# A three-pass graph kernel whose first pass gathers raw node rows and normalises them per edge, in place of a table of normalised rows

## The chip, the cores and the metric

The kernel runs on one core of one Trainium2 chip. The metric is device time in microseconds (us), the median of several runs. Beside the timed runs there is one profiled execution, whose trace gives the start and length of every instruction. The engines are named as in the profile: PE (matrix products; PEld is its weight load), DVE (vector), ACT (activations), POOL (GpSimd), SP (issues transfers). Indirect transfers ("gathers": 128 rows picked by 128 indices) are issued by POOL.

## The reference

Two graph layers over 30,000 nodes of 128 features and 960,000 edges sorted by destination. Each layer normalises the node rows and applies a Relu before its messages.

```python
h = jnp.maximum(_layernorm(x, axis=-1), 0.0)
x = x + _L0_gnn_ref(h, edge_weight1, basis1, coeff1, bias1, basis2, coeff2, bias2,
                    src, dst, edge_type_32)      # two convolutions, Relu between
h = jnp.maximum(_layernorm(x, axis=-1), 0.0)
x = x + _L1_gnn_ref(h, edge_index, edge_type_4, Wk, bk, Wq, bq, Wv, bv, Ws, b)
```

A convolution of layer 0 sends, along each edge, the source row times the weight of the edge's type (a mix of eight basis matrices by `coeff`), times the edge's own weight, and sums at the destination. Layer 1 sends `sigmoid(k[dst] + q[src]) * v[src]`.

## The kernel before, in words

The edges are cut into 7,500 tiles of 128; three tiles make a group (G = 3), five groups a step (S = 5), five steps a load stage (SB = 5); below, "stage" in the estimates means one step of five groups. There are 500 steps per pass, 100 load stages, and NI = 5 long blocks, unrolled. Edges run from the highest destination to the lowest, so that a group's destinations lie in a window of W = 32 nodes above its first one. Sums are kept in SBUF in `agg`, one column per node (128 x 30360).

**Preparation** (lines 186 to 312). `agg` is set to zero on POOL (L177). 25 steps of 1,200 nodes load x on SP (L230), take statistics on DVE (bn_stats L236, then four small steps L239 to L244), a square root on ACT (L249), reciprocal and shift on DVE (L251, L253), and scale and Relu the rows on ACT (L265), two rows in ten on POOL (L260, L263) from the sixth step on; the rows are stored to the table h0 in HBM (L267). In between, five chunks subtract each group's first destination from its destinations (L205), store these positions to `reld` (L214) and take their lowest and highest (L213, L217). From these a count of violations is summed through PE into `flag` and loaded into a register of every engine (L312). If it is zero, the sorted path runs (L1079), otherwise a general path.

**Sorted path**, three passes of `edge_pass` (L404), each with 7,500 gathers:

- Passes 1 and 2 (`rel_body`, L479). Per group: three gathers of source rows into one slot of `hg` (L598 to L600, issued through L118; five slots); `sb` = position one-hot (`hits`, L592) times the edge's eight coefficients (L604, DVE); three products on PE into `pa` (L608), the first of which waits for all three gathers; a copy by ACT to `ab` (L619). Per step: 16 products with the bases (`bases_out`, L562), emitted after the next step's second group; window sums into `agg` (L477, DVE). In pass 1 also the edge types' one-hot `oh` (L526), their product with the coefficients (L531) and the scaling by the edge weights (`ce`, L541). Pass 1 also turns finished blocks of 120 nodes into h1 (`after_first`, L731), and prepares codes for pass 3 (`codes`, L866).
- Pass 2 gathers from h1, pass 3 (`gate_body`, L643) gathers query and value rows and multiplies them out.

The order inside the blocks is the order of emission, written by hand (`tc.manual_schedule()`); small steps are put beside given groups by `todo` and `beside`. Every engine works its instructions in that order. A slot is reused when what read and wrote it is done.

Of the kernel before, what the change touches and what calls it, by code (L numbers as in the profile page):

```python
# [52 lines left out]
CH = 5  # L53
PX, KX = 120, 10
BUSY = 5
# [17 lines left out]
def kernel(  # L73
# [103 lines left out]
    nc.gpsimd.memset(agg, 0.0)  # L177
# [4 lines left out]
    bas1 = state.tile([P, B, D], F32, name="bas1")  # L182
# [3 lines left out]
    CT, CG = NT // CH, NGR // CH  # L186
    STEPS = N // (PX * KX)
    with tc.tile_pool(name="prep", bufs=2) as prep, tc.tile_pool(name="pre", bufs=4) as pre, \
            tc.tile_pool(name="prep_ps", bufs=1, space=PSUM) as prep_ps:
        lo = prep.tile([TP, CH], F32, name="lo", bufs=1)  # L190
        hi = prep.tile([TP, CH], F32, name="hi", bufs=1)

        def edge_chunk(c):

            ts = slice(c * CT, (c + 1) * CT)
            fi = prep.tile([TP, CG], I32, name="fi")
            dch = prep.tile([TP, CT], I32, name="dch")
            rch = prep.tile([TP, CT], BF16, name="rch")

            def load():  # L200
                nc.sync.dma_start(fi, rows_of(first[c * CG:(c + 1) * CG], TP))
                nc.sync.dma_start(dch, dst[:, ts])

            def less():
                nc.vector.tensor_tensor(  # L205
                    rch.rearrange("p (g j) -> p g j", j=G),
                    dch.rearrange("p (g j) -> p g j", j=G),
                    fi.unsqueeze(2).to_broadcast([TP, CG, G]),
                    ALU.subtract,
                )  # L210

            def lowest():
                nc.vector.tensor_reduce(lo[:, c:c + 1], rch, AX.X, ALU.min)  # L213
                nc.scalar.dma_start(reld[:, ts], rch)  # L214

            def highest():
                nc.vector.tensor_reduce(hi[:, c:c + 1], rch, AX.X, ALU.max)  # L217

            return load, less, lowest, highest

        xts, sums, scales, shifts = {}, {}, {}, {}

        def rows(array, i):
            some = array[i * (PX * KX):(i + 1) * (PX * KX), :]
            return some.rearrange("(p k) d -> p k d", k=KX)

        def load(i):
            if i < STEPS:
                xts[i] = pre.tile([PX, KX, D], F32, name="xt", bufs=5)
                nc.sync.dma_start(xts[i], rows(x, i))  # L230

        def statistics(i):
            if i < STEPS:
                st = pre.tile([PX, KX, 6], F32, name="st")
                for k in range(KX):
                    nc.vector.bn_stats(st[:, k, :], xts[i][:, k, :])  # L236
                even, odd = (st[:, :, q * 3 + 1:q * 3 + 3] for q in range(2))
                sums[i] = pre.tile([PX, KX, 2], F32, name="mv")
                nc.vector.tensor_add(sums[i], even, odd)  # L239
                apart = pre.tile([PX, KX], F32, name="apart")  # L240
                nc.vector.tensor_sub(apart, even[:, :, 0], odd[:, :, 0])
                nc.vector.scalar_tensor_tensor(apart, apart, D / 4.0, apart,
                                               op0=ALU.mult, op1=ALU.mult)
                nc.vector.tensor_add(sums[i][:, :, 1], sums[i][:, :, 1], apart)  # L244

        def scale(i):
            if i < STEPS:
                scales[i] = pre.tile([PX, KX], F32, name="rs")
                nc.scalar.activation(scales[i], sums[i][:, :, 1], AF.Sqrt, scale=1.0 / D,  # L249
                                     bias=eps[:PX])  # L250
                nc.vector.reciprocal(scales[i], scales[i])  # L251
                shifts[i] = pre.tile([PX, KX], F32, name="off")
                nc.vector.scalar_tensor_tensor(shifts[i], sums[i][:, :, 0], -0.5, scales[i],  # L253
                                               op0=ALU.mult, op1=ALU.mult)

        def results(i):
            h = pre.tile([PX, KX, D], F32, name="h", bufs=3)
            own = KX if i < BUSY else KX - 2
            for k in range(own, KX):
                nc.gpsimd.tensor_scalar(h[:, k, :], xts[i][:, k, :], scales[i][:, k:k + 1],  # L260
                                        shifts[i][:, k:k + 1], op0=ALU.mult, op1=ALU.add)
            if own < KX:
                nc.gpsimd.tensor_scalar(h[:, own:], h[:, own:], 0.0, None, op0=ALU.max)  # L263
            for k in range(own):
                nc.scalar.activation(h[:, k, :], xts[i][:, k, :], AF.Relu,  # L265
                                     scale=scales[i][:, k:k + 1], bias=shifts[i][:, k:k + 1])
            nc.scalar.dma_start(rows(h0, i), h)  # L267

        def edge_steps():
            ready = edge_chunk(0)  # L270
            yield ready[0]
            for c in range(CH):
                following = edge_chunk(c + 1) if c + 1 < CH else ()
                yield from following[:1]
                yield from ready[1:]
                ready = following

        with tc.manual_schedule():
            between = edge_steps()
            for i in range(4):  # L280
                load(i)
            statistics(0)
            scale(0)
            statistics(1)
            for i in range(STEPS):
                load(i + 4)
                if i == STEPS - 5:
                    nc.sync.dma_start(bas1, basis1.rearrange("b d f -> d b f"))
                statistics(i + 2)
                scale(i + 1)  # L290
                next(between, int)()
                results(i)
            for step_ in between:
                step_()
        bad = prep.tile([TP, 2, CH], F32, name="bad", bufs=1)
        nc.vector.tensor_scalar(bad[:, 0, :], lo, 0.0, None, op0=ALU.is_lt)
        nc.vector.tensor_scalar(bad[:, 1, :], hi, float(W - 1), None, op0=ALU.is_gt)
        nbad = prep.tile([TP, 1], F32, name="nbad", bufs=1)
        nc.vector.tensor_reduce(nbad, bad, AX.XY, ALU.add)
        at = prep.tile([NI, NG], I32, name="at", bufs=1)  # L300
        nc.sync.dma_start(at, first.rearrange("(i g) -> i g", i=NI))
        even = prep.tile([NI, NG], F32, name="even", bufs=1)
        nc.gpsimd.iota(even, pattern=[[-NPI // NG, NG]], base=N + LAG - LEAD - W,
                       channel_multiplier=-NPI, allow_small_or_imprecise_dtypes=True)
        nc.vector.tensor_tensor(even, at, even, ALU.is_gt)
        late = prep.tile([NI, 1], F32, name="late", bufs=1)
        nc.vector.tensor_reduce(late, even, AX.X, ALU.add)
        nc.vector.tensor_add(nbad[:NI], nbad[:NI], late)
        pbad = prep_ps.tile([1, 1], F32, name="pbad")
        nc.tensor.matmul(pbad, lhsT=nbad, rhs=ones[:TP], start=True, stop=True)  # L310
        nc.vector.tensor_copy(flag, pbad)
    n_bad = nc.values_load(flag[0:1, 0:1], min_val=0, max_val=2 * CH * TP + NGR)  # L312
# [44 lines left out]
    def sorted_path():  # L357
# [7 lines left out]
        with ExitStack() as all_:  # L365
# [38 lines left out]
            def edge_pass(name, body, after, banks, extra=None, finish=None, apart=None):  # L404


                with ExitStack() as held:
                    weights = held.enter_context(tc.tile_pool(name=f"{name}_w", bufs=1))
                    steps, start = after(weights), body(weights)
                    with tc.tile_pool(name=f"{name}_io", bufs=4) as io, \  # L410
# [10 lines left out]
                        for i in range(NI):  # L421
                            with tc.manual_schedule():
                                todo = {}
                                for n, step_ in extra(i, npool) if extra else ():
                                    todo.setdefault(n, []).append(step_)
# [53 lines left out]
            def rel_body(table, weights, second):  # L479
# [3 lines left out]
                def start(npool):  # L483
                    bas = weights
                    if second:
                        bas = npool.tile([P, B, D], F32, name="bas")
                        nc.scalar.dma_start(bas, weights.rearrange("b d f -> d b f"))
# [15 lines left out]
                def body(bas, pos, hits, i, io, pool, ps, cp, iw, ic, beside):  # L503
# [5 lines left out]
                    def loads(k):  # L509
                        stage[k] = [stage_tile(io, "idx", src, I32, i, k),  # L510
                                    stage_tile(io, "relc", reld, BF16, i, k),
                                    firsts(io, i, k)]
                        if not second:
                            stage[k].append(
                                stage_tile(io, "nrm", norm, F32, i, k, 4 * TQ - S * G))
# [55 lines left out]
                    if second:  # L571
                        kept(0)
                        kept(1)
                    else:
                        types(0)
                        onehot(0)
                        coefficients(0)
                        types(1)
                        onehot(1)
# [564 lines left out]
```

## Time and profile before

| | us |
|---|---|
| median of 3 runs | 28303.81 (28299.06 to 28304.94) |
| the profiled execution | 28301.08 |
| its span | 28299.3 |
| busy: PE, DVE, ACT, POOL | 19712.1, 11533.8, 3619.0, 21324.8 |
| gathers into hg (passes 1 and 2) | 15000 x 945 ns |
| gathers into qv (pass 3) | 7500 x 945 ns |
| granted PE clock, mean over the span | 0.751 |

The span runs from the first to the last instruction. A row of a group of instructions names the line, the engine, the operation and the tiles, out from in, with the shapes; then the count, the busy time, the mean of one in ns, and the idle time of the engine before them with what ended it ("issue" is time in which the engine waited for nothing that the profile shows). A row in order of time has the start, the length, engine, line, operation, tiles and count, and in brackets the idle time before. A queue's own rows end in q (SPq, ACTq).

### The profile page before, as it was taken

Reading aid. Unit: us, or ns where it says so; the run is one execution under the profiler, and the core shown is the slowest. Engines: PE = TensorE matmul, PEld = TensorE weight load, DVE = VectorE, ACT = ScalarE, POOL = GpSimd, SP = SyncE. Lnnn points to the kernel's source line nnn. Section 1 sums busy time; section 2 is a strip of 40 time slices with the busy share of each in tenths; the row PEclk is TensorE's granted clock in tenths of the full one; section 3 lists DMA queues with packets and bytes.
Section 4 is the critical chain, followed back from the end, with each engine's and each line's share of the span. In section 5 each row is a group of like instructions: output and inputs, shape, how many; then the busy total and the mean of one; then the engine's idle time right before and its main releaser. Section 6 shows DMA issues by size and latency. Waiting matters only on the chain.

```text
span 28299.3 us, 269530 instructions
## 1 busy us (share of the span) xinstructions
PE 19712.1 (70%) x79371; PEld 15934.8 (56%) x79371; DVE 11533.8 (41%) x23522; ACT 3619.0 (13%) x9761; POOL 21324.8 (75%) x22574
## 2 busy tenths in 40 slices
PE   5666666666666666666666666667777777777777
PEld 4555555555555444444444444457777777777676
DVE  4333333333333333333333333344444444444444
ACT  2111111111111111111111111111111111111111
POOL 7777777777777777777777777777777777777777
PEclk9888888888888888888888888875555555555555
DMA  4222222222222222222222222235555555555554
GB/s 126 75 75 83 75 81 77 75 84 74 77 81 75 74 77 76 76 77 77 77 77 77 77 77 76 76 101 151 151 152 152 151 152 152 152 151 152 152 152 146
DMA packets 1982721, 2911.61 MB, mean 103 GB/s; under 512 B 680564, under 2 KB 1364077, under 8 KB 1981277
## 3 DMA queue, kind: packets, MB, share of 16 engines
q0 software_dynamic: 840000, 1967.52, 24.7%
q1 hardware_dynamic: 740695, 656.22, 7.5%
q10 hardware_dynamic: 400582, 270.54, 3.6%
q8 instruction: 672, 11.01, 0.2%
q14 instruction: 772, 6.32, 0.1%
HBM read 2621.06 MB, written 271.38 MB: 102 GB/s over the span
## 4 chain that ended last, share of the span: by engine, by line
POOL 36%; DMA 31%; issue 23%; PE 6%; DVE 2%; DVEq 0%; POOLq 0%; ACT 0%; SPq 0%; ACTq 0%
DMA hg<-h,idx 24%; POOL hg L118 22%; POOL qv L118 14%; DMA qv<-qvtab,qi 7%; PE pa L608 3%; PE pb L562 2%; DVE pk L715 1%; DVE msg L687 1%; DVE agg L477 0%; PE bank L806 0%; PE cp L531 0%; DVEq L464 0%; DVE sb L604 0%; POOLq L118 0%; PE po L689 0%
## 5 line engine op out<-in xcount | busy, mean ns | idle before, releaser
L118 POOL DMA_INDIRECT hg<-h,idx x15000 | 14168.1, 945 | 4592.9 <-issue 3623.0
L608 PE MATMUL pa<-sb,hg 128*128 128x256 f32 x30000 | 8716.0, 435 | 6192.4 <-DMA hg<-h,idx 4946.6
L608 PEld LDWEIGHTS pa<-sb,hg 128*128 128x128 f32 x30000 | 5983.7, 212 | 8490.9 <-issue 5744.2
L118 POOL DMA_INDIRECT qv<-qvtab,qi x7500 | 7090.1, 945 | 2312.9 <-issue 2055.2
L689 PE MATMUL po<-sel,msg 128*128 128x32 f32 x15000 | 3653.5, 400 | 2206.9 <-DVE msg L687 2202.0
L689 PEld LDWEIGHTS po<-sel,msg 128*128 128x128 f32 x15000 | 3401.0, 327 | 2799.8 <-DVE msg L687 2795.0
L678 PE MATMUL pk<-kw,oh 128*128 128x128 f32 x15000 | 4029.8, 442 | 11.4 <-DMA kw<-ktab 11.4
L619 ACT COPY ab<-pa 128x256 f32<-128x256 f32 x5000 | 1860.3, 372 | 16488.9 <-PE pa L608 16205.4
L678 PEld LDWEIGHTS pk<-kw,oh 128*128 128x128 f32 x15000 | 3504.1, 334 | 11.6 <-issue 11.6
L715 DVE TENSOR_TENSOR pk<-pk,qv 128x384 f32<-128x384 f32 x2500 | 1415.7, 566 | 5017.4 <-DMA qv<-qvtab,qi 4627.3
L477 DVE TENSOR_TENSOR agg<-agg,pb 128x32 f32 x5000 | 937.4, 187 | 4488.3 <-PE pb L562 4342.8
L562 PE MATMUL pb<-ab,bas 128*128 128x160 f32 (+1 forms) x12080 | 2705.0, 387 | 0.9 <-ACT ab L619 0.9
L562 PEld LDWEIGHTS pb<-ab,bas 128*128 128x128 f32 x12080 | 2352.3, 230 | 399.0 <-issue 58.6
L604 DVE TENSOR_TENSOR sb<-hits,ce 128x768 f32<-128x768 f32 x2500 | 2295.1, 950 | 192.7 <-issue 167.3
L604 DVE TENSOR_TENSOR sb<-cp,ce 128x768 f32<-128x768 f32 x2500 | 2308.1, 948 | 17.2
L716 ACT ACTIVATE pk<-pk 128x384 f32<-128x384 f32 x2500 | 1187.5, 475 | 8056.7 <-DVE pk L715 8056.7
L789 DVE BATCH_NORM_STATS2 st<-bank 120x6 f32<-120x128 f32 x253 | 75.6, 299 | 3339.8 <-PE bank L786 3339.8
L687 DVE TENSOR_TENSOR msg<-pk,qv 128x384 f32<-128x384 f32 x2500 | 1369.3, 548 | 0.0
L665 DVE TENSOR_TENSOR oh<-kb,cp 128x1920 f32<-128x1920 bf16 x500 | 1072.3, 2145 | 7.8 <-DMA kb<-kcode 7.8
L817 DVE TENSOR_TENSOR kt<-bank,ball 120x512 f32<-120x512 f32 x253 | 175.0, 692 | 1795.4 <-PE bank L806 1795.1
L806 PE MATMUL bank<-wall,hT 128*120 128x512 f32 x1518 | 836.1, 665 | 0.0
L592 DVE TENSOR_TENSOR hits<-cp,relc 128x480 f32<-128x480 f32 x500 | 330.7, 661 | 693.1 <-PE cp L531 691.0
(87 smaller groups left out, 5371.5 us busy)
## 6 DMA issues: line engine op xcount, KB each, us to landing
hg<-h,idx POOLq DMA_INDIRECT x15000
kb<-kcode SPq DMA_DIRECT2D x500, 480.0 KB
kw<-ktab SPq DMA_DIRECT2D x2500, 64.0 KB
er<-in_et_row SPq DMA_DIRECT2D x500, 256.0 KB
qvtab<-qvt ACTq DMA_DIRECT2D x250, 480.0 KB
qv<-qvtab,qi POOLq DMA_INDIRECT x7500
ktab<-kt ACTq DMA_DIRECT2D x253, 240.0 KB
ce<-ce ACTq DMA_DIRECT2D x500, 60.0 KB
```

Source lines behind the costliest of these rows:

```text
L118: return nc.gpsimd.indirect_dma_start(out=to, out_offset=None, in_=table, in_offset=bass.IndirectOffsetOnAxis(ap=idx, axis=0))
L477: nc.vector.tensor_add(to, to, po[:, at + g, :])
L562: nc.tensor.matmul(po[z][:, of].rearrange("p s w -> p (s w)"), lhsT=bas[:, b, :], rhs=ab[z][:, b, of].rearrange("p s w -> p (s w)"), start ...
L604: nc.vector.tensor_mul(sb, hits[:, of, :].unsqueeze(2).to_broadcast([TP, G, B, W]), ce[s][:, of, :].unsqueeze(3).to_broadcast([TP, G, B, W]))
L608: product = nc.tensor.matmul(pa.rearrange("p b w -> p (b w)"), lhsT=hg[:, j, :], rhs=sb[:, j].rearrange("p b w -> p (b w)"), start=(j == 0 ...
L619: nc.scalar.copy(ab[z][:, :, s % A * S + g, :], pa)
L665: nc.vector.tensor_tensor(oh[s], kb[s], ic.unsqueeze(2).to_broadcast([P, S, GE]), ALU.is_equal)
L678: nc.tensor.matmul(pk[n][:, j, :], lhsT=oh[n // S][:, n % S, j * TP:(j + 1) * TP], rhs=kw[n], start=True, stop=True)
L687: nc.vector.tensor_mul(msg, pk[n], qv[n][:, :, 1, :])
L689: nc.tensor.matmul(po[s][:, g, :], lhsT=msg[:, j, :], rhs=sel[s][:, g * G + j, :], start=(j == 0), stop=(j == G - 1))
L715: nc.vector.tensor_add(pk[n], pk[n], qv[n][:, :, 0, :])
L716: nc.scalar.activation(pk[n], pk[n], AF.Sigmoid)
```

## The change

The preparation goes, and with it the table h0 on the sorted path. Pass 1 gathers rows of x itself, into seven slots instead of five. Its groups are handled in two batches of a step, groups 0 and 1, and groups 2, 3 and 4. When a group's rows are there, DVE takes their statistics; when the batch's last are, DVE combines them, ACT takes the square root of the spread for all the batch's tiles, DVE makes reciprocal and shift, and ACT scales and Relus the rows in place, three tiles at a time, each three followed by the group's three products and ACT's copy. The first product no longer waits for all rows of its group in pass 1. Positions are made at the load stages, 75 columns at a time, from loads of the destinations and of the groups' first destinations; they are used from SBUF in pass 1 and stored for the later passes. Their extremes are kept per load stage. `agg` is cleared by DVE in 25 pieces beside the first 25 groups. The count of violations is made in pass 2 beside its 62nd to 64th group; it is loaded into registers between passes 2 and 3. The sorted path always runs, and the general path follows after it if the count is above zero; that path now makes h0 for itself.

```diff
+BATCHES = {1: (0, 1), 4: (2, 3, 4)}
+CLEARED = 25
...
-    nc.gpsimd.memset(agg, 0.0)
...
-    with tc.tile_pool(name="prep", bufs=2) as prep, tc.tile_pool(name="pre", bufs=4) as pre, \
-            tc.tile_pool(name="prep_ps", bufs=1, space=PSUM) as prep_ps:
...
-    n_bad = nc.values_load(flag[0:1, 0:1], min_val=0, max_val=2 * CH * TP + NGR)
+    STAGES = NI * NQ
+    lo = state.tile([TP, STAGES], F32, name="lo")
+    hi = state.tile([TP, STAGES], F32, name="hi")
...
                     def loads(k):
...
+                            dch = stage_tile(io, "dch", dst, I32, i, k)
+                            fi = io.tile([TP, NGS], I32, name="fi")
+                            n = i * NG + k * NGS
+                            nc.sync.dma_start(fi, rows_of(first[n:n + NGS], TP))
...
+                    def positions(k):
+                        dch, fi = stage[k][1]
+                        relc = io.tile([TP, NTS], BF16, name="relc")
+                        nc.vector.tensor_tensor(
+                            relc.rearrange("p (g j) -> p g j", j=G),
+                            dch.rearrange("p (g j) -> p g j", j=G),
+                            fi.unsqueeze(2).to_broadcast([TP, NGS, G]), ALU.subtract)
+                        stage[k][1] = relc
+                        n = i * NQ + k
+                        nc.scalar.dma_start(reld[:, n * NTS:(n + 1) * NTS], relc)
+                        nc.vector.tensor_reduce(lo[:, n:n + 1], relc, AX.X, ALU.min)
+                        nc.vector.tensor_reduce(hi[:, n:n + 1], relc, AX.X, ALU.max)
+
+                    def statistics(st, hg):
+                        for j in range(G):
+                            nc.vector.bn_stats(st[:, j, :], hg[:, j, :])
+
+                    def spread(st, n):
+                        even, odd = (st[:, :n, q * 3 + 1:q * 3 + 3] for q in range(2))
+                        both = pool.tile([TP, 3 * G, 2], F32, name="both")[:, :n]
+                        nc.vector.tensor_add(both, even, odd)
+                        apart = pool.tile([TP, 3 * G], F32, name="apart")[:, :n]
+                        nc.vector.tensor_sub(apart, even[:, :, 0], odd[:, :, 0])
+                        nc.vector.scalar_tensor_tensor(apart, apart, D / 4.0, apart,
+                                                       op0=ALU.mult, op1=ALU.mult)
+                        nc.vector.tensor_add(both[:, :, 1], both[:, :, 1], apart)
+                        rs = pool.tile([TP, 3 * G], F32, name="rs")[:, :n]
+                        nc.scalar.activation(rs, both[:, :, 1], AF.Sqrt, scale=1.0 / D,
+                                             bias=eps[:TP])
+                        return both, rs
+
+                    def shifted(both, rs, n):
+                        nc.vector.reciprocal(rs, rs)
+                        off = pool.tile([TP, 3 * G], F32, name="off")[:, :n]
+                        nc.vector.scalar_tensor_tensor(off, both[:, :, 0], -0.5, rs,
+                                                       op0=ALU.mult, op1=ALU.mult)
+                        return off
...
+                        if not second and s % SB == SB - 1 and k + 1 < NQ:
+                            positions(k + 1)
...
                         for g in range(S):
-                            hg = pool.tile([TP, G, D], F32, name="hg", bufs=5)
+                            hg = pool.tile([TP, G, D], F32, name="hg", bufs=5 if second else 7)
                             rows = [gather(hg[:, j, :], table, idx[:, t0 + j:t0 + j + 1])
                                     for j in range(G)]
+                            ready = BATCHES.get(g)
+                            if not second:
+                                if g in (0, 2):
+                                    st = pool.tile([TP, 3 * G, 6], F32, name="st")
+                                at = (g if g < 2 else g - 2) * G
+                                statistics(st[:, at:at + G], hg)
+                                if ready:
+                                    both, rs = spread(st, at + G)
                             sb = pool.tile([TP, G, B, W], F32, name="sb", bufs=4)
...
+                            held[g] = hg, rows, sb
+                            if second:
+                                product(g, *held[g])
+                            elif ready:
+                                off = shifted(both, rs, at + G)
+                                for q, one in enumerate(ready):
+                                    for j in range(G):
+                                        n = q * G + j
+                                        mine = held[one][0][:, j, :]
+                                        nc.scalar.activation(mine, mine, AF.Relu,
+                                                             scale=rs[:, n:n + 1],
+                                                             bias=off[:, n:n + 1])
+                                    product(one, *held[one])
...
+            def clear(q):
+
+                size = NX // CLEARED
+                low = NX - (q + 1) * size if q + 1 < CLEARED else 0
+                return lambda: nc.vector.memset(agg[:, low:NX - q * size], 0.0)
...
+                return [(61, count), (62, ahead), (63, whole)]
...
-            edge_pass("c1", rel_body(h0, bas1, False), after_first, 2, codes, finish_later)
-            edge_pass("c2", rel_body(h1, basis[1], True), after_second, 2, apart=6)
+            edge_pass("c1", rel_body(x, basis[0], False), after_first, 2, codes, finish_later)
+            edge_pass("c2", rel_body(h1, basis[1], True), after_second, 2, verdict, apart=6)
             both.close()
+            n_bad = nc.values_load(flag[0:1, 0:1], min_val=0,
+                                   max_val=2 * STAGES * TP + NGR)
             edge_pass("g", lambda weights: lambda cps: gate_body, after_third, 1)
...
-    with tc.If(n_bad == 0) as cmp:
-        sorted_path()
-    with cmp.Else():
+    n_bad = sorted_path()
+    with tc.If(n_bad > 0):
         any_path()
```

`product` holds the three products and ACT's copy that stood in the loop before.

## The prediction

> **What bounds the kernel now.** I read the page first, then a table by stage, cut at the first and last gather of each pass, then what GpSimd (POOL) waits for in pass 1, then the instructions in order of time around the places that the change touches. From the page: the span, the chain that ended last, and the costliest group.
>
> ```profile
> span 28299.3 us, 269530 instructions
> ...
> POOL 36%; DMA 31%; issue 23%; PE 6%; DVE 2%; DVEq 0%; POOLq 0%; ACT 0%; SPq 0%; ACTq 0%
> ...
> L118 POOL DMA_INDIRECT hg<-h,idx x15000 | 14168.1, 945 | 4592.9 <-issue 3623.0
> ```
>
> Gathers (POOL issues, their DMAs, POOL's "issue" gap) carry the chain. By stage (length, then busy time and instructions of PE, weight loads, DVE, ACT, POOL, then the granted clock):
>
> ```profile
> 0.00:128.50 128.50, 0.19 (x2) 0.09 (x2) 97.80 (x427) 90.96 (x236) 66.64 (x74) 1.00 0.88 299
> 128.50:9505.70 9377.20, 6114.54 (x27478) 5056.94 (x27478) 3514.24 (x7312) 1045.26 (x2999) 7091.77 (x7500) 0.86 0.28 78
> 9505.70:9518.50 12.80, 4.97 (x28) 3.85 (x28) 4.86 (x14) 2.00 (x7) 0.00 (x0) 0.91 0.24 56
> 9518.50:18880.20 9361.70, 6403.51 (x21554) 4286.52 (x21555) 3625.65 (x7235) 1190.84 (x3498) 7076.29 (x7500) 0.89 0.28 77
> ```
>
> Each pass issues 7,500 gathers. In pass 1 they start at a mean pitch of (9504.74 - 128.50)/7499 = 1.2503 us: 0.946 busy and 0.304 of gap. What POOL waited for there (total, times, longest):
>
> ```profile
> POOL hg L118 <- issue: 1808.2, 5933, 0.3
> POOL hg L118 <- DMA hg<-h,idx: 390.1, 1280, 0.3
> POOL hg L118 <- PE pa L608: 47.5, 156, 0.3
> POOL hg L118 <- PE cp L531: 34.7, 114, 0.3
> POOL hg L118 <- DMA h<-h: 9.2, 1, 9.2
> ```
>
> Apart from the first gather (9.2 us, for the normalised rows) no wait is longer than the fixed gap of 0.3 us: buffers, PE, DVE and ACT never hold POOL up. So the span is the time before the first gather, three lots of 7,500 pitches, two transitions and a tail. Only what moves the first gather, the pitch or a transition moves the end. POOL's rows there:
>
> ```profile
> 128.50 1.15 POOL L118 DMA_INDIRECT hg<-h,idx  x1 [9.25 <-DMA h<-h]
> 129.96 0.94 POOL L118 DMA_INDIRECT hg<-h,idx  x1 [0.30 <-issue]
> ...
> 9504.74 0.94 POOL L118 DMA_INDIRECT hg<-h,idx  x1 [0.30 <-issue]
> 9518.55 0.94 POOL L118 DMA_INDIRECT hg<-h,idx  x1 [12.88 <-DVE sb L604]
> ```
>
> **Start.** The table of normalised rows goes, and with it all work up to 128.50 us: 25 loads and 25 stores of 600 KB, statistics, ACT's and POOL's scaling, five large position chunks. The first gather then needs only its indices, SP's first DMA. SP issued its first at 0.74 us, an index load takes 0.36 us to issue, and the last small store before pass 2 was issued by 9515.83, 2.7 us before the gather that it released. 0.74 + 0.36 + 2.7 = 3.8; POOL's constants end at 2.2. I take 4.0, bounds 3.5 to 6.5 (the first 600 KB load was used at 6.11). **-124.5 us**, between -125.0 and -122.0.
>
> **POOL in pass 1.** It loses a memset (25.4 us, which lay beside the old preparation) and gains no data work. A slot of hg must now also be free of DVE's and ACT's accesses, so there are more waits in POOL's queue. The trace shows one extra wait instruction per group there already (17 ns, once 804 ns of waiting at 310.96), with the next gather still 1.25 us after the one before; the first eight gathers had none, at the same pitch. I take 0; dearer only if a wait outlasts about 0.8 us.
>
> **ACT in pass 1**, per stage of 5 groups = 15 gathers = 18.75 us. Added: 15 Relus and two square roots. From the preparation and the steady part of pass 1 (start, length):
>
> ```profile
> 86.96 3.17 ACT L265 ACTIVATE h<-xt,off,rs 120x128 f32<-120x128 f32 x8
> ...
> 326.01 1.53 PE L608 MATMUL pa<-sb,hg 128*128 128x256 f32 x6 [3.04 <-DMA hg<-h,idx]
> ...
> 327.58 0.37 ACT L619 COPY ab<-pa 128x256 f32<-128x256 f32 x1 [4.20 <-PE pa L608]
> 327.85 0.40 ACT L746 ACTIVATE r<-agg,b1c 128x120 f32<-128x120 f32 x1
> ...
> 341.25 2.90 PE L608 MATMUL pa<-sb,hg 128*128 128x256 f32 x6 [3.20 <-DMA hg<-h,idx]
> ```
>
> Eight Relus in 3.17 us at 479 ns each are a pitch of 0.385. The written order is three Relus, PE's products, ACT's copy of the sum, then the next group's Relus, so ACT and PE take turns. At full clock: first Relu 0.48 + 0.05 + products 1.57 to the copy's start + 0.27 to ACT's next = 2.4 us. At half clock the products took 2.90: 3.8 us. Five groups, plus per batch about 0.9 us (square root 0.30, then DVE's reciprocal 0.21 and shift 0.17 with their gaps), plus 0.85 for ACT's stores and other steps: 12.0 + 1.8 + 0.85 = **14.6 us of 18.75** at full clock, **21.6** at half. The granted clock of pass 1 is 0.86, half clock 28% of the time: 5 x 2.8 + 2.65 = 16.6. It fits. Behind a late batch stand the next batch's square root, hence DVE's shift and whatever DVE has queued behind it; POOL feels that only when a slot stays full.
>
> **Slots.** Count from a stage's first gather. Group 4's last row lands at 14 x 1.25 + 2.2 = 19.7 (the row issued at 323.80 met its product at 326.01). Statistics 0.3, DVE's four small steps 0.75, sb 0.95 beside the square root, shift 0.45: first Relu near 22. Group 2 is then multiplied by 24.4 (25.5 at half clock). Its slot, with seven, is wanted at 9 x 3.75 = 33.8: 8 to 9 us of slack. That covers a slow batch, which falls behind by about 3 x 1.4.
>
> **DVE in pass 1.** Now 3514.2/500 = 7.0 us a stage. Added: 15 statistics at a pitch of 0.20 (ten took 2.02) = 3.0, two batches of small steps 2.4, positions under 0.2 (three short instructions per five stages): 12.6 of 18.75. The 25 clears come in the first 25 groups: the 64-column memset took 112 ns and the one-column 59, so 0.84 ns a column, 1214 columns = 1.07 us, 5.3 a stage: 18 of 18.75 over five stages. What is late next at the start is the first product: ACT issues the eight coefficient loads until 9.34, the two one-hot products (1.94 each there, at half clock) and hits end near 17, the first Relus near 21, the first product near 24, and slot 0 is wanted at 4 + 7 x 3.75 = 30. Cover: the slots. I take **+2 us** for stalls there, bounds 0 and 10.
>
> **DVE against POOL.** 139 gathers of pass 1 took over 0.955 us, 15.3 us together above 0.944; pass 2 has 0.2. Of these, 84 stand beside an oh row (L526) alone, 9.6 us; the kr, sx and kc rows (60 in all) account for about 2.5, 0.04 each. oh is the one large DVE row of a faster kind: 512 elements in 492 ns, where hits takes 661 for 480. bn_stats (128 in 277 ns) is of the slower kind, as ce (128 in 280) is, and ce never stands alone beside a long gather. Of the new two-input steps there are ten a stage, 0.17 us against sx's 0.55: at most 5,000 x 0.04 x 0.3 = 65 us; nearest the ce row it is nothing. Below nothing, the 15 us could vanish if rows fall elsewhere. I take **+10**, bounds -15 and 65.
>
> The Trainium skill, "SBUF — State Buffer", section on the shared port pair, speaks against this change: a Vector instruction with two SBUF inputs, or in a two-port mode, holds GpSimd off until it ends. Read as a lock on whole instructions it would give an estimate of 5,000 x 0.17 = 850 us at worst; the 2,500 sb rows beside gathers show nothing of that size.
>
> **End of pass 1.** Now: last row landed about 9506.9, copy 9509.0 to 9509.4, next pass's gather 9518.55. After, three groups follow the last landing: 2.5 us to the first Relu, then 2 x 2.4 + 2.5 = 7.3, so the copy ends at 9516.7 on the same clock (9520.9 at half): **+8.5**, bounds 7.3 and 12.7 with half-clock bases.
>
> **Registers.** The value that decides the general path is loaded on every engine between passes 2 and 3; SP's took 1.35 us, and SP stands in that transition's chain (POOL is idle there 28.2 us anyway): **+1.5**, 0 to 2. The other moves lie beside POOL's pitch: a few DVE steps and one product for the verdict, at two groups' distance; its iota on POOL (0.54) ahead of pass 2, inside POOL's 12.9 us of idle; on SP one more small load per five stages (0.3 to 0.45 to issue, SP being idle most of the time); on ACT one store of positions (0.4) per five stages, in the 0.85 above.
>
> **Sum:** -124.5 + 2 + 10 + 8.5 + 1.5 = -102.5. The profiled execution took 28301.08 (1.8 beyond its span), 2.7 below the median of 28303.81: 28303.8 - 102.5 = **28201 us**. Bounds together: -125 - 15 + 7.3 = -133, and -122 + 10 + 65 + 12.7 + 2 = -32: 28171 to 28272.
>
> **Rivals.** (a) *ACT and PE become the bound of pass 1 (slower).* With 5c + 2.65 > 18.75, c over 3.22, that is with 59% of the products at half clock, pass 1 runs at ACT's pace; at 100% it is 21.6, (21.6 - 18.75) x 500 - 100 = +1,325: 29,630; at 70%, 19.5, +275: 28,580. For it: pass 3 sits at clock 0.50 throughout with PE 76% busy, and in the turns PE idles 0.8 us a group. Against: after each first batch the 16 base products follow at once (3.75 us at half clock, 6.6 with the group before), and in pass 1 a stretch of 3.4 us filled without a gap is followed by full clock; a late PE has no gaps. Chance 0.12.
> The Trainium skill, "TensorE: Matmul & The Clock Gate", Part 1, gives that window as about 3.4 us of sustained work, and the fall to half rate after as long an idle one; by it the gap between batches is the danger, and only that.
> (b) *The gathers lengthen beside DVE (no change).* 50 us needs 0.007 us a gather; with 50 to 65 us and slow transitions the time is 28,247 to 28,272. For it the L526 row, against it ce, sb and hits. Chance 0.07.
> (c) *The preparation comes back as a slow start:* clears and the first constants keep DVE behind, POOL waits 20 to 60 us in the first 100. The change then does only half of what it says: 28,220 to 28,260. Chance 0.06, half of it within 0.2%.
>
> Forecast 0.75. Faster by over 0.2% (57 us, about what a measurement can tell) 0.78, within 0.2% 0.10, slower 0.12. The range is the sum of the bounds, 28171 to 28272, and leaves (a) and the end of (b) out.
>
> **What would show it.** First gather at 3.5 to 6.5 us; POOL's waits in pass 1 still 0.3 at longest, pitch 1.250 to 1.259; ACT busy near 8.6 us a stage; granted clock of pass 1 above 0.75; gather to gather 20 to 26 us between passes 1 and 2. Wrong if POOL waits on PE or ACT in pass 1, if gathers average over 0.955, or if the clock there falls to 0.5.

## The result, and the profile after

The changed kernel takes 30550.86 us (median of 4 runs, 30535.78 to 30555.64), the kernel before beside it 28304.38 us: a ratio of 1.0793, 95% interval 1.078 to 1.0807. The forecast was 28201 us with 28171 to 28272 around it. The change is slower by 7.9%, far outside.

The page of the changed kernel, in the same order as before: span, the chain that ended last, the costliest groups.

```profile
span 30548.2 us, 289281 instructions
...
PE 0%; DMA 0%; DVE 0%; issue 0%; ACT 0%; POOL 0%; ACTq 0%; DVEq 0%
...
L520 PE MATMUL pa<-sb,hg 128*128 128x256 f32 x30000 | 10330.8, 494 | 7018.4 <-ACT hg L560 4078.3
...
L118 POOL DMA_INDIRECT hg<-in_x,idx x7500 | 7082.2, 944 | 4640.8 <-PE pa L520 2838.7
```

The chain of waits could not be followed back here (all shares are 0%), so the stages have to carry the reading. The groups already tell where to look: in pass 1 a gather still takes 944 ns, but POOL now stands idle 4640.8 us before them, and PE's products (`product`, L520) end most of that. Cut at the gathers as before:

```profile
0.00:3.16 3.16, 0.00 (x0) 0.00 (x0) 0.19 (x3) 0.00 (x0) 1.42 (x12) 1.00 0.18 26
3.16:11725.20 11722.04, 7642.77 (x27432) 5609.22 (x27432) 5885.99 (x21109) 4318.72 (x11473) 7082.16 (x7500) 0.73 0.23 63
11725.20:11767.29 42.09, 25.20 (x75) 18.32 (x74) 9.99 (x41) 12.16 (x34) 0.54 (x1) 0.62 0.09 25
11767.29:21129.40 9362.11, 6400.70 (x21553) 4279.72 (x21554) 3629.73 (x7244) 1191.90 (x3498) 7076.60 (x7500) 0.89 0.28 77
```

The preparation is gone and pass 2 is what it was. Pass 1 is 11722.04 long instead of 9377.20, and no engine fills it: POOL is busy 60%, PE 65%, DVE 50%, ACT 37%. A stage in which nobody is full and everybody waits points to a loop of waits. POOL's waits in it:

```profile
POOL hg L118 <- PE pa L520: 2838.7, 1741, 9.6
POOL hg L118 <- issue: 1760.5, 5656, 9.5
POOL hg L118 <- DMA hg<-in_x,idx: 25.1, 81, 0.7
```

Waits of up to 9.6 us for a slot stand where none behind the first gather was longer than 0.3. Laid out by the gathers (us; the last three columns are experiments told below):

| | before | changed | sums first | extra products | no normalisation |
|---|---|---|---|---|---|
| first gather | 128.5 | 3.2 | 3.2 | 3.1 | 3.2 |
| pass 1, first to last gather | 9376.2 | 11721.1 | 9411.2 | 9867.5 | 9386.3 |
| granted clock in it | 0.864 | 0.729 | 0.853 | 0.962 | 0.849 |
| on to pass 2's first | 13.8 | 43.0 | 22.2 | 31.6 | 16.9 |
| pass 2 | 9360.7 | 9361.1 | 9362.9 | 9361.1 | 9361.4 |
| on to pass 3's first | 29.2 | 28.5 | 28.4 | 29.2 | 28.3 |
| pass 3 | 9373.8 | 9374.3 | 9375.8 | 9374.0 | 9374.0 |
| span | 28299.3 | 30548.2 | 28220.7 | 28683.2 | 28186.9 |

So -125.3 at the start, +2344.8 in pass 1, +29.2 behind it: nearly all of the +2248.9. A step of pass 1 (15 gathers) takes 23.46 us on average (steps 20 to 490) instead of 18.75. One such step in order of time (start, length, engine and line, in brackets the idle time before and who ended it):

```profile
5030.81 1.26 ACT L560 ACTIVATE hg<-hg,off,rs 128x128 f32<-128x128 f32 x3 [0.46 <-DVE off L429]
...
5033.77 1.56 PE L520 MATMUL pa<-sb,hg 128*128 128x256 f32 x6 [0.85 <-ACT hg L560]
...
5035.18 2.34 PE L478 MATMUL pb<-ab,bas 128*128 128x160 f32 x16
...
5037.62 1.08 DVE L351 TENSOR_TENSOR agg<-agg,pb 128x32 f32 x5 [1.77 <-PE pb L478]
...
5038.61 0.67 DVE L410 BATCH_NORM_STATS2 st<-hg 128x6 f32<-128x128 f32 x3
...
5040.09 0.30 ACT L422 ACTIVATE rs<-both,eps 128x9 f32<-128x9 f32 x1 [4.04 <-DVE both L420]
...
5041.22 1.26 ACT L560 ACTIVATE hg<-hg,off,rs 128x128 f32<-128x128 f32 x3 [0.83 <-DVE off L429]
...
5041.76 2.93 PE L520 MATMUL pa<-sb,hg 128*128 128x256 f32 x6 [3.20 <-ACT hg L560]
...
5044.97 0.95 POOL L118 DMA_INDIRECT hg<-in_x,idx  x1 [3.71 <-PE pa L520]
...
5045.55 2.93 PE L520 MATMUL pa<-sb,hg 128*128 128x256 f32 x6 [0.85 <-ACT hg L560]
...
5053.25 0.30 ACT L422 ACTIVATE rs<-both,eps 128x6 f32<-128x6 f32 x1 [0.42 <-ACT h L699]
```

Read it as a relay. ACT and PE take turns for the first batch (two groups). The 16 base products follow. DVE's window sums (L351) wait for these, and only then come the statistics (L410) of the fifth group, since they stand behind the sums in DVE's written order. The five sums are those of step s-2, whose base products were long done; but both halves of the PSUM tile `pb` are one tile, and in the order of emission the base products of step s-1 have written to it last. With the statistics come the small steps, ACT's square root, shift, Relus, and the second batch's three turns, here with products of 2.93 us (half clock). Behind the last turn ACT takes the next first batch's square root, and the next step begins, 23.2 us after this one's (5030.05). Nothing in the ring waits for rows: by the medians over steps 20 to 490 the fifth group's last gather was issued 5.9 us before the step's first Relu, its statistics start 9.5 us behind that Relu.

DVE's waits in pass 1 show the two sides of the ring, the sums for PE and the first batch's reciprocal for ACT:

```profile
DVE rs L427 <- ACT rs L422: 2937.4, 499, 7.9
DVE agg L351 <- PE pb L478: 2400.0, 487, 7.4
```

In the kernel before, the sums already waited so:

```profile
DVE agg L477 <- PE pb L562: 4293.8, 490, 14.2
```

There DVE had nothing urgent behind them; this looked like DVE's idle time, and was a wait at a fixed place in its order.

### The profile page after: what moved, and what is told of

Its sections match the earlier page's. It is cut to its first block, busy times and chain, and to the rows that moved or that the text cites. A ratio compares the mean times of both kernels' runs of the same rounds, so it can differ in the third digit from the quotient of the medians.

```text
span 30548.2 us, 289281 instructions
## 1 busy us (share of the span) xinstructions
PE 21253.8 (70%) x79371; PEld 16494.8 (54%) x79371; DVE 13817.7 (45%) x36932; ACT 6813.1 (22%) x18026; POOL 21251.2 (70%) x22513
## 5 line engine op out<-in xcount | busy, mean ns | idle before, releaser
L520 PE MATMUL pa<-sb,hg 128*128 128x256 f32 x30000 | 10330.8, 494 | 7018.4 <-ACT hg L560 4078.3
L520 PEld LDWEIGHTS pa<-sb,hg 128*128 128x128 f32 x30000 | 6738.3, 241 | 10342.8 <-ACT hg L560 5387.0
L118 POOL DMA_INDIRECT hg<-in_x,idx x7500 | 7082.2, 944 | 4640.8 <-PE pa L520 2838.7
L118 POOL DMA_INDIRECT hg<-h,idx x7500 | 7076.6, 944 | 2292.3 <-issue 1870.7
L560 ACT ACTIVATE hg<-hg,off,rs 128x128 f32<-128x128 f32 x7500 | 3155.4, 485 | 657.2 <-DVE off L429 645.3
L478 PE MATMUL pb<-ab,bas 128*128 128x160 f32 (+1 forms) x12080 | 2571.1, 372 | 0.9 <-ACT ab L531 0.9
L478 PEld LDWEIGHTS pb<-ab,bas 128*128 128x128 f32 x12080 | 2203.6, 216 | 387.0 <-issue 56.7
L548 DVE TENSOR_TENSOR sb<-hits,ce 128x768 f32<-128x768 f32 x2500 | 2363.3, 945 | 52.1 <-PE pa L520 50.1
L351 DVE TENSOR_TENSOR agg<-agg,pb 128x32 f32 x5000 | 937.5, 187 | 2634.4 <-PE pb L478 2461.4
L410 DVE BATCH_NORM_STATS2 st<-hg 128x6 f32<-128x128 f32 x7500 | 1677.0, 279 | 167.7 <-issue 146.0
L427 DVE RECIPROCAL rs<-rs 128x6 f32<-128x6 f32 x1000 | 198.2, 198 | 2948.9 <-ACT rs L422 2945.3
```

Source lines behind the costliest of these rows:

```text
L118: return nc.gpsimd.indirect_dma_start(out=to, out_offset=None, in_=table, in_offset=bass.IndirectOffsetOnAxis(ap=idx, axis=0))
L410: nc.vector.bn_stats(st[:, j, :], hg[:, j, :])
L478: nc.tensor.matmul(po[z][:, of].rearrange("p s w -> p (s w)"), lhsT=bas[:, b, :], rhs=ab[z][:, b, of].rearrange("p s w -> p (s w)"), start ...
L520: made = nc.tensor.matmul(pa.rearrange("p b w -> p (b w)"), lhsT=hg[:, j, :], rhs=sb[:, j].rearrange("p b w -> p (b w)"), start=(j == 0), ...
L548: nc.vector.tensor_mul(sb, hits[:, of, :].unsqueeze(2).to_broadcast([TP, G, B, W]), ce[s][:, of, :].unsqueeze(3).to_broadcast([TP, G, B, W]))
L560: nc.scalar.activation(mine, mine, AF.Relu, scale=rs[:, n:n + 1], bias=off[:, n:n + 1])
```

## The experiments

The theories. **Closed ring**: the sums' wait ties the second batch's statistics to the first batch's products; turns, base products, sums, statistics, turns follow one another in every step (the expectations call it the order theory, or the closed chain). **Turns** (the prediction's rival (a)): ACT and PE in turns at half clock are too slow by themselves. **Slots**: seven slots are too few. The first four kernels ran on a chip on which the kernel before itself took 33,301 us. In the trace of e1 from there PE waits over 3 us 517 times in 9,900 us of pass 2 (12,000 to 21,900), in the changed kernel's whole pass 2 four times. The four kernels are compared with one another and with the kernel before there, and were run again elsewhere.

**e1, e1b: sums first.** The sums of step s-2 go to the start of the step, ahead of all its statistics.

```diff
+                        if not second and s > 1:
+                            sums(s - 2)
                         for g in range(S):
...
-                            if not second and g == 3 and s > 1:
-                                sums(s - 2)
```

> One edit to the changed kernel: in pass 1 the window sums of step s-2 are emitted ahead of the step's first group instead of after its fourth. Order theory: in the changed kernel these sums wait for the base products of step s-1 (sums start 8.17 us after the first Relu of the first batch, the base products end at 8.06), because both halves of pb are one tile, and the fourth and fifth groups' statistics stand behind them on DVE; so every step is one chain of 23.5 us (first batch, base products, sums, statistics, second batch). With the sums early they wait only for products of a step before; the chain is cut, pass 1 is left with ACT and PE taking turns, 5 x 3.2 + 2.65 = 18.7 us a step at the measured mix of clocks: 28,200 to 28,700 us. Turns theory (rival (a) of the prediction, ACT and PE alternating at half clock is the bound by itself): the turns are unchanged, so at most the sums' 1.1 us a step goes: 29,600 to 30,550.

Measured: ratio 1.0025 (1.0016 to 1.0035).

**e2, e2b: Relus first.** All Relus of a batch, then all its products: ACT and PE no longer take turns.

```diff
                                 for q, one in enumerate(ready):
                                     for j in range(G):
...
+                                for one in ready:
                                     product(one, *held[one])
```

> One edit to the changed kernel: all Relus of a batch are emitted before the batch's products and copies, so that PE works a batch through without waiting for ACT between groups. Turns theory: three of the five turns go (0.85 us of PE idle each), PE fills the clock's windows and leaves half clock (products 1.56 instead of 2.93): under 18.75 us a step, 28,200. Order theory: the chain of a step stays, shortened: first batch 3.7 + base products 2.4 + sums 1.1 + statistics to first Relu 3.1 + second batch 5.7 + 0.7 = 16.7 at full clock, 24 at half; at a mix of clocks 19 to 21: 28,300 to 29,400, POOL waiting on PE in some steps.

Measured: 1.1051 (1.1028 to 1.1073).

**e3, e3b: both.**

> The edits of e1_sums_early and e2_relus_first together. Both theories: pass 1 goes back to POOL's pitch of 1.250 us, no wait of POOL over 0.4 us in its steady part, and the start that was gained is kept: 28,190 to 28,230 us (first gather near 3.2 us instead of 128.5, some 20 to 25 us instead of 13.8 between passes 1 and 2).

Measured: 0.9996 (0.9986 to 1.0006).

**e4, e4b: ten slots** (`bufs=5 if second else 10`).

> One edit to the changed kernel: ten slots for the gathered rows instead of seven. Slots theory (a batch holds its slots too long for seven): POOL's waits go, 28,200 to 28,700. Order and turns theories: the step is a closed chain of 23.5 us that no buffer shortens; POOL only runs three groups further ahead before it waits: 30,450 to 30,560.

Measured: 1.1009 (1.0987 to 1.1031). On this chip the kernels split in two: with the sums first, as long as the kernel before (33,385 and 33,291 us); with the sums' wait left in, 10% longer (36,797 and 36,660). There the sums' place alone tells the two groups apart, and neither the turns nor the slots do. The sizes say nothing of the undisturbed chip, so the kernels were run again on one (before: 28305.25), with the changed kernel beside them.

> The changed kernel as it is, as the reference of this call. The first call ran on a chip on which the kernel before took 33,301 us, with PE standing still for 3 to 10 us about every 20 us in all three passes, so its times can't be set beside 28,304. On an undisturbed chip: 30,550 us, steps of pass 1 of 23.5 us.

Measured: 30565.22 us, 1.0799 (1.0777 to 1.082).

> The same edit as e1_sums_early: in pass 1 the window sums of step s-2 ahead of the step's first group. Order theory: the chain through the base products is cut, POOL's pace or nearly so, 28,200 to 28,700 on an undisturbed chip; where the kernel before takes longer, a ratio below 1.02 against 1.08 or more for the changed kernel. Turns theory: at most 1.1 us a step of the 4.7 lost: 29,900 to 30,550.

Measured: 28222.52 us, ratio 0.9971 (0.9959 to 0.9983). One edit of the order takes back the whole loss. The turns by themselves are not too slow: they are written as in the changed kernel, and the loss is gone. From this kernel's trace, at the same place in a step (its Relus are L562):

```profile
5015.36 2.93 PE L520 MATMUL pa<-sb,hg 128*128 128x256 f32 x6 [0.85 <-ACT hg L562]
...
5018.08 3.88 PE L478 MATMUL pb<-ab,bas 128*128 128x160 f32 x16
...
5018.70 0.30 ACT L422 ACTIVATE rs<-both,eps 128x9 f32<-128x9 f32 x1
...
5019.49 1.26 ACT L562 ACTIVATE hg<-hg,off,rs 128x128 f32<-128x128 f32 x3 [0.49 <-DVE off L429]
...
5022.63 1.51 PE L520 MATMUL pa<-sb,hg 128*128 128x256 f32 x6
```

The second batch's square root runs 0.6 us into the base products, and its first Relus are done before these end. PE goes from the base products (and the one-hot products behind them) to the next group's without waiting for ACT, and full clock is back (1.51 after 3.88 and 2.93). On average 1.3 of the five sets of products per step are at half clock, against 3.0 in the changed kernel. DVE now waits for rows, that is, for POOL:

```profile
DVE rs L427 <- ACT rs L422: 1468.6, 595, 7.9
DVE st L410 <- DMA hg<-in_x,idx: 1224.4, 1272, 3.4
```

> The same edit as e2_relus_first: all Relus of a batch ahead of its products and copies, the sums where they were. Turns theory: back to POOL's pace, 28,200. Order theory: the closed chain of a step stays; it shortens only as far as PE comes back to full clock, 28,300 to 29,800, and POOL still waits on PE.

Measured: 28234.93 us, 0.9975 (0.9965 to 0.9986). This is below what the closed ring expected, and to be explained: the ring is still closed (its sums start 0.1 us behind the base products, the statistics of the fifth group behind the sums), but without the turns it is shorter, and a step takes 18.86 us, POOL's pace with small waits. So the ring costs only what it is longer than POOL's 18.75, and either cut is enough on an undisturbed chip: the turns do have a part in the loss, as a piece of the ring. That e2 lost 10% on the other chip would fit, since a closed ring of about POOL's pace has nothing left for a stall; no run shows this by itself.

> The same two edits as e3_both. Both theories: pass 1 at POOL's pitch of 1.250 us, the gained start kept: 28,190 to 28,230 us on an undisturbed chip, faster than the kernel before by some 0.3%.

Measured: 28231.29 us, 0.9974 (0.9964 to 0.9984). The two cures don't add.

The last four ran together on an undisturbed chip (before: 28306.04).

> Ten slots of gathered rows in the first pass instead of seven, all else as in the change. Theory of the closed chain (statistics of a step's last groups behind the window sums on DVE, the sums behind the base products on PE): rows already lie ready about 13 us before they are used, so more slots cannot shorten a step; 30,450 to 30,600 us, step period 23.2 to 23.7 us. Theory of the slots (seven are too few, POOL waits for a slot and the rows come late): 28,200 to 29,300 us.

Measured: 30528.64 us, 1.0792 (1.0774 to 1.081). The fifth group's last gather is now issued 20.7 us before the step's first Relu (5.9 with seven slots), and the step still takes 23.4. The slots are not it.

**e8: sums last** (`g == 4` in place of `g == 3` before the sums, behind the last statistics and shift).

> The window sums of the step before last go behind the statistics and shift of the step's last group on DVE, not to the start of the step. Theory of the closed chain: any place at which no statistics stand behind the wait for the base products opens it, so 28,210 to 28,260 us, pitch of pass 1 1.252 to 1.260. Rival, that the early place itself was what helped (sums of agg lie beside other accesses there): no better than 29,500.

Measured: 28222.36 us, 0.997 (0.9959 to 0.9982), pitch 1.2558. Not the early place helps, but that no statistics stand behind the wait.

**e7: extra products** that keep PE busy between base products and second batch.

```diff
+WARM = 12
...
+                            if not second and g == 3:
+                                for q in range(WARM):
+                                    nc.tensor.matmul(cp[:, 64:192], lhsT=ident,
+                                                     rhs=bas[:, q % B, :], start=True, stop=True)
```

> As the change, with twelve more products on PE per step of pass 1, between the base products and the products of the step's last three groups; nobody reads them. They fill the stretch in which PE waits for statistics, square root and shift. If the half clock lengthens the chain: at full clock the three products take 1.56 us instead of 2.93, 2.99 of the five sets per step were at half clock, so 23.46 - 2.99 x 1.37 = 19.4 us per step, bounds 18.9 to 20.3: 28,260 to 29,000 us, granted clock of pass 1 above 0.9. If the chain is long for another reason than the clock: 30,000 or more (12 products more cannot shorten it).

Measured: 28697.36 us, 1.0143 (1.0126 to 1.016). Pass 1 by stage, and the ring at full clock (lines are one further here):

```profile
3.11:9871.50 9868.39, 7119.45 (x39411) 5743.80 (x39412) 5905.81 (x21109) 4321.08 (x11477) 7094.67 (x7500) 0.96 0.29 75
```

```profile
5014.44 2.34 PE L479 MATMUL pb<-ab,bas 128*128 128x160 f32 x16
...
5016.82 1.07 DVE L352 TENSOR_TENSOR agg<-agg,pb 128x32 f32 x5 [3.09 <-PE pb L479]
5017.45 2.90 PE L575 MATMUL cp<-bas,ident 128*128 128x128 f32 x24
5017.81 0.67 DVE L411 BATCH_NORM_STATS2 st<-hg 128x6 f32<-128x128 f32 x3
5019.22 0.30 ACT L423 ACTIVATE rs<-both,eps 128x9 f32<-128x9 f32 x1 [4.21 <-DVE both L421]
...
5020.96 1.35 PE L521 MATMUL pa<-sb,hg 128*128 128x256 f32 x5 [0.61 <-ACT hg L561]
```

Twelve products more per step, and the kernel takes 6% less time than the changed one. The ring is still closed (the sums start 0.07 us behind the last base product in the median, as in the changed kernel), but the clock is 0.96 and the step takes 19.74 us. So of the 4.71 us by which a changed step exceeds 18.75, 0.99 is the ring at nearly full clock and 3.72 is the half clock that the ring's idle stretches bring. Most of that, 3.6 us, comes from the sets of products: 2.62 fewer a step are at half clock, and a set is 1.37 us shorter at full. In medians, (1.0799 - 1.0143) of (1.0799 - 0.9971): four fifths.

**e5: no normalisation.** Statistics, square root, shift and Relus are left out of pass 1, so the result is another one. A group's products follow its own gathers, and the first again waits for all three, as in the kernel before.

> Leaves the normalisation of the gathered rows out of pass 1 (no statistics, square root, shift, scaling or Relu there: the products take the raw rows); everything else of the change stays. What is left should keep POOL's pace whatever the theory: 28,180 to 28,215 us. It sizes what the normalisation costs once the chain is open: against the run with the sums at the start of the step (28,222.5) the difference should be 10 to 40 us, in gathers lengthened beside DVE and in the end of pass 1 (about 7). If the long gathers come from the steps that were there before (oh), they stay above 150 here; if from the statistics, they fall to about 140.

Measured: 28184.8 us, 0.9957 (0.994 to 0.9973). The rest of the change is worth 121 us; the normalisation costs 38 of it when the ring is open (e8 beside it).

## Why the prediction was wrong, point by point

- **Start** -124.5: -125.3 in the changed kernel. The first gather starts at 3.17, the clears take 1.07 us each. The +2 for early stalls is seen where the ring doesn't cover them: in e1b POOL waits over 0.35 us twice in pass 1, both times within its first 150 gathers, and loses 2.9 us.
- **ACT in pass 1**: the step that failed, with its sentence "It fits". The pieces were right: ACT is busy 4318.72/500 = 8.64 us a step (8.6 expected), and a turn is 2.41 us at full and 3.78 at half clock (2.4 and 3.8). They were added up as one load of ACT and PE in turns, 16.6 us, and held against 18.75. Steps with load to spare can still form a ring, and the ring's length is not any engine's load. It was not walked round: base products to sums, sums to the statistics behind them on DVE, statistics to square root. "Behind a late batch stand the next batch's square root, hence DVE's shift and whatever DVE has queued behind it" followed the queue one way, from ACT to DVE; what stands *ahead* of the statistics on DVE, and what that waits for, was not asked. e1b and e8 move only this, and the forecast's size appears. In the changed kernel the fifth group's statistics start 9.5 us behind the step's first Relu and a step takes 23.46; in e1b they start 3.6 us behind it and a step takes 18.82 (median and mean over steps 20 to 490).
- **The clock mix** was taken from the pass before (28% of the time at half clock). The ring makes its own: 60% of the products. The gap between the base products and the second batch's first product, 3.2 us in the step shown, is what rival (a)'s "a late PE has no gaps" passed over; e7 fills it.
- **Rival (a)** had the sign and the danger (half clock) but not the mechanism: by its formula 60% at half clock is 5 x 3.23 + 2.65 = 18.8 us a step, no loss; measured 23.46. e1b has the same turns and no loss.
- **Slots**: "8 to 9 us of slack", held to cover a slow batch. A slack is spent once; a ring that is 4.7 us too long takes that from it in every step. e4b: more slots, the same time.
- **DVE's load** 12.6 us a step: 5885.99/500 = 11.8.
- **DVE against POOL** +10, bounds -15 and 65: to be seen only with the ring open. In e1b pass 1 is 35.0 longer than before; gathers over 0.955 us are 263 and exceed 0.944 by 45.0 us together (before: 139, 15.3), so 29.7 is theirs, three times the +10 forecast, and of the rest 2.9 the early stalls'. That is far from the 850 us that the prediction estimated for a lock on whole instructions. In e5, without normalisation, 205 of them and 25.0: a third of the rise comes with the rest of the change. In all three kernels most lie beside an `oh` row (115, 181, 226), in e1b most beside a row of statistics too (239); why the same `oh` row meets a long gather more often (18%, 31%, 43% of the gathers beside it) stays open.
- **End of pass 1** +8.5: +8.4 in e1b; +29.2 in the changed kernel, where the backlog is worked off behind the last gather.
- **Registers** +1.5: -0.6.
- **What would make it wrong** was named rightly: "if POOL waits on PE or ACT in pass 1"; and the clock, 0.729, is below the 0.75 given.

With the sums moved, the kernel takes 28222.5 us against the 28201 forecast, inside its range: 83 us (0.3%) faster than the kernel before. No version with the full computation here is faster beyond the noise (e8: 28222.4). The start, the early stalls and the end of pass 1 came out about as forecast; the lengthened gathers, 29.7 in place of 10, are most of the 21 us between. What is shown: the sums' wait, the statistics behind it and the clock's part. That the sums wait because the two halves of `pb` count as one tile is read from the code and the trace's releaser; two tiles were not tried, so this reason stays unshown.

## What to carry to other kernels

Before work on a critical path is put on an engine that looks idle, look at the waits of that engine's other instructions: what stands ahead of the new work in the written order, and what does *that* wait for. Then walk from the new work back to itself; if the walk closes within one step, its length must be below the step, at half clock too, whatever the engines' loads add up to. Where a ring is closed, moving the waiting instruction can open it and leave the new work as it is.

## What the runs showed of the hardware that was not expected

The clock holds on to its state. The traces of pass 1, cut into windows of 3.41 us on the clock's own edges, by PE's busy share in a window and whether the clock changed at its end:

| pass 1 | before | changed |
|---|---|---|
| half clock, busy under 0.7: to full | 0 of 305 | 0 of 456 |
| half clock, 0.7 to 0.8 | 0 of 64 | 38 of 910 |
| half clock, 0.8 to 0.9 | 40 of 48 | 250 of 273 |
| half clock, 0.9 and more | 326 of 331 | 218 of 218 |
| full clock, busy under 0.4: to half | 284 of 284 | 371 of 371 |
| full clock, 0.4 to 0.6 | 82 of 693 | 136 of 581 |
| full clock, 0.6 and more | 0 of 1014 | 0 of 615 |

A turn at half clock, 2.93 us of products and 0.85 of waiting, is 78% busy: in this pass too little, in nearly all windows, to bring full clock back, while the same turn at full clock (1.56 and 0.85, 65%) keeps it. So the same instructions have two lasting paces, and in the changed kernel a gap of some 3 us (3.3 in the median step) takes PE from one to the other; with that gap filled (e7) the clock stays at 0.96. The Trainium skill, "TensorE: Matmul & The Clock Gate", Part 1, has the window of about 3.4 us, which these edges show; that a pattern without any long gap stays at half rate is what the table adds.

The shares hold for this pass. In pass 3 of the kernel before, with other products, PE was busy 0.9 or more in 485 windows at half clock, and full clock followed 4 of them; the clock stays at 0.50 there (behind the length: PE, weight loads, DVE, ACT, POOL, clock):

```profile
18908.40:28283.20 9374.80, 7164.36 (x30226) 6571.68 (x30226) 4275.86 (x8485) 1282.84 (x2999) 7090.07 (x7500) 0.50 0.52 152
```

So PE's busy share as the profile shows it does not decide alone. What differs in pass 3 was not tried.
